# The first expert block's rows, put together on TensorE from the tiles in SBUF instead of read back from DRAM

## The chip, the cores and the metric

The kernel runs on one core of a Trainium2 chip. Its time is the time of the whole launch on the device, in microseconds; lower is better. The kernel before was timed in three runs; the median is what counts. One more execution was taken with the hardware profiler on, and all rows of a profile quoted here come from such an execution.

A core has five engines that run their own instruction streams side by side: PE (TensorE, matrix products; PEld is its weight load), DVE (VectorE), ACT (ScalarE), POOL (GpSimd) and SP (SyncE, which here only issues DMA transfers). They wait for each other by semaphores. SBUF is the core's on-chip memory of 128 partitions, PSUM the memory that PE writes its products to.

## The reference, cut to what matters

Four sequences of 512 tokens with 256 channels. First a gated cross-attention: each token has an index `seg_id` into a context and looks at the four context rows ending there (16 heads of 16 channels). Then a mixture of experts: a gate picks the two best of eight experts for each token.

```python
x = x + tanh(g_xattn[0]) * xattn(layernorm(x), ctx_1024, seg_id, Wq, Wkv, Wo)
# the experts' part, on n = layernorm(x):
gate_probs = softmax(n @ gate_w.T)              # 8 experts
top_v, top_i = top_k(gate_probs, 2)
for e in range(8):
    h = silu(n @ w1[e] + b1[e])                 # 256 -> 1024
    y = h @ w2[e] + b2[e]                       # 1024 -> 256
    out = out + y * comb_w[..., e:e+1]          # top_v where e was picked, else 0
x = x + tanh(g_ffn[0]) * out
```

All data are 32-bit floats.

## The kernel before, in words

**Tiles.** The 2048 tokens are 16 tiles of 128. A tile goes through four stages. `rows_of` has POOL gather its context rows (L240, three buffers). `stage_ask` makes the query: PE `pq` (L426), ACT copies the gate's part (L430). `stage_attend` is DVE work: `prod` (L439, 1024 elements in each partition), its sums (L442), the softmax with ACT's exponent (L459), `v` (L472, written over a buffer of the same kind as `prod`), and sums into `ao` (L483, L485). `stage_out` has PE transpose `ao` (`pa`, L497 or L499), ACT copy it (L512), PE multiply by the output matrix (`po`, L515), and DVE add into `x_sb` (L518) and compute moments for the second normalisation.

**Routing.** Tiles are routed in groups of 2, 2, 1, 1, 1, 1, 2, 2, 2, 2 tiles. `stage_route` stores the tile's `x` (SP, L537), finds the two best experts of each token (DVE; `pick`, L562), counts with two products `pp` over `pick` (L568, L571) how many earlier tokens picked the same expert, and so gives each token a place: `pos` (L604 to L606), a row number in a DRAM array `xs`, which has one region for each expert. ACT takes the exponent for the gate (`exg`, L592) and writes the normalised rows (L609); two scatters on POOL for each tile send them to `xs` (L377). Each row also carries, for each expert, the weight of its result and its token number.

**Queue.** After five tiles (`RAMP`), and after each further group, `queue(i, w)` (L660 to L738) works out, from counts that PE sums (`pn`, L666), which blocks of 128 rows of one expert are sure to be full by now, and which expert and first row each of the next `w` blocks has. DVE does this in some twenty small instructions. Three blocks (0, 1, 2) are sure after five tiles, two more after each of tiles 5, 6 and 7, four more after each pair that follows. 37 blocks are run.

**Blocks.** For each block SP reads the expert and the row number, loads the first-layer weight (`w1s`, L752, three buffers, 1 MB), the biases (L756, L758), the rows `xg` (L770) and their weights `ms` (L773); a load of rows waits until all scatters that can hold its rows have landed. PE transposes the rows (`pxg`, L783), DVE copies them to SBUF (`xgT`, L786), PE makes the hidden layer (`ph`, L798, 32 matrix records), ACT applies Silu (L810, eight instructions), PE makes the result (`py`, L825, 16 records), DVE scales it (`yw`, L836) and POOL adds it to the tokens' rows in the output (L839, an indirect DMA that adds).

**Who sets the order.** The program is written as tiles first, blocks after; a scheduler at build time sorts each engine's instructions by their dependencies and priorities, so attention and blocks interleave on PE, ACT, POOL and SP, in an order that is fixed before the kernel starts. DVE's order for the tiles' part is the written one (`in_order`). In the main loop at index `i` this is: the first half of tile `i`'s attention, the output stage of tile `i - 1`, the question of tile `i + 1`, the routing of the group that ends at `i`, the queue, then (for `i` from 5 on) the rest of tile `i`'s attention:

```python
if i >= RAMP and queued:
    queue(i, queued - before)
    before = queued
...
if i in (0, RAMP, RAMP + 2):
    normalise_first(1 + (i + 1) // TPB)
for _ in attend:
    pass
```

At `i == RAMP` (5) tiles 0 to 4 have been routed and the first three blocks are known; the rest of tile 5's attention follows on DVE.

Of the kernel before, what the change touches and what calls it, by code (L numbers as in the profile page):

```python
# [9 lines left out]
F32 = mybir.dt.float32  # L10
I32 = mybir.dt.int32
U32 = mybir.dt.uint32
AF = mybir.ActivationFunctionType
ALU = mybir.AluOpType
AX = mybir.AxisListType

P = 128
KW = 4
# [5 lines left out]
def gated_xattn_moe(  # L24
# [25 lines left out]
    nc = tc.nc  # L50
    NTOK, D = x.shape
# [3 lines left out]
    KD = D // P  # L55
# [112 lines left out]
    def iota_f(name, shape, pattern, base=0, cm=0):  # L168
        t_i = const.tile(shape, I32, name=name + "_i")
        nc.gpsimd.iota(t_i, pattern=pattern, base=base, channel_multiplier=cm)  # L170
        t_f = const.tile(shape, F32, name=name)
        nc.gpsimd.tensor_copy(t_f, t_i)
        return t_f
# [4 lines left out]
    jfull = iota_f("jfull", [P, NJ], [[P, NJ]], base=P)  # L178
    jany = iota_f("jany", [P, NJ], [[P, NJ]], base=1)
    sid = iota_f("sid", [P, NS], [[1, NS]])  # L180
    srow = iota_f("srow", [P, NS], [[P, NS]])
    tokid = const.tile([P, NT + 1], I32, name="tokid")
    nc.gpsimd.iota(
# [168 lines left out]
    def _layers(ctx, is_near):  # L352
# [18 lines left out]

        scatters, reads = [], []

        def scatter(rows, where):
# [56 lines left out]
        def stage_attend(t):  # L433

            pq = ops.pop(t)
            gt = gathered.pop(t)
            prod = att.tile([P, KW, D], F32, tag="prod", name=f"prod_{t}", bufs=3)
            sc = small.tile([P, KW, H], F32, tag="sc", name=f"sc_{t}")
            seen[t] = nc.vector.tensor_tensor(  # L439
                prod, pq[:, 0:D].unsqueeze(1).to_broadcast([P, KW, D]), gt[:, :, 0:D], ALU.mult  # L440
            ).ins
            nc.vector.tensor_reduce(  # L442
                sc.rearrange("p o h -> p (o h)"),
                prod.rearrange("p o (h d) -> p (o h) d", d=HD),
                AX.X,
                ALU.add,
            )
            yield

            nc.vector.tensor_tensor(  # L450
                sc, sc, neg[:, t, :].unsqueeze(2).to_broadcast([P, KW, H]), ALU.add
            )
            mx = small.tile([P, H], F32, tag="mx", name=f"mx_{t}")
            nc.vector.tensor_reduce(mx, sc.rearrange("p o h -> p h o"), AX.X, ALU.max)
            nc.vector.tensor_tensor(
                sc, sc, mx.unsqueeze(1).to_broadcast([P, KW, H]), ALU.subtract
            )
            ex = small.tile([P, KW, H], F32, tag="ex", name=f"ex_{t}")
            exps[t] = nc.scalar.activation(ex, sc, AF.Exp, scale=rsa[:, t : t + 1]).ins  # L459
            yield  # L460
            sm = small.tile([P, H], F32, tag="sm", name=f"sm_{t}")
            nc.vector.tensor_reduce(sm, ex.rearrange("p o h -> p h o"), AX.X, ALU.add)
            rc = small.tile([P, H], F32, tag="rc", name=f"rc_{t}")
            nc.vector.reciprocal(rc, sm)
            pr = small.tile([P, KW, H], F32, tag="pr", name=f"pr_{t}")
            nc.vector.tensor_tensor(
                pr, ex, rc.unsqueeze(1).to_broadcast([P, KW, H]), ALU.mult
            )
            yield

            v = att.tile([P, KW, D], F32, tag="prod", name=f"v_{t}", bufs=3)
            nc.vector.tensor_tensor(  # L472
                v.rearrange("p o (h d) -> p o h d", d=HD),
                gt[:, :, D : 2 * D].rearrange("p o (h d) -> p o h d", d=HD),
                pr.unsqueeze(3).to_broadcast([P, KW, H, HD]),
                ALU.mult,
            )
            if t + 1 < RAMP:

                ops[t] = v  # L480
                yield
                return
            nc.vector.tensor_add(v[:, 0:2, :], v[:, 0:2, :], v[:, 2:4, :])  # L483
            ao = att.tile([P, 1, D], F32, tag="ao", name=f"ao_{t}")
            nc.vector.tensor_add(ao[:, 0, :], v[:, 0, :], v[:, 1, :])  # L485
            ops[t] = ao
            yield
# [42 lines left out]
        def stage_route(g):  # L530
# [70 lines left out]
            nc.vector.tensor_tensor(  # L601
                hot, hot, place.unsqueeze(2).to_broadcast([P, GT, TOPK, E]), ALU.mult
            )
            pos = gate.tile([P, GMAX, TOPK], I32, tag="pos", name=f"pos_{g}")[:, 0:GT]  # L604
            with nc.allow_low_precision("row numbers"):
                nc.vector.tensor_reduce(pos, hot, AX.X, ALU.add)  # L606
            nc.vector.scalar_tensor_tensor(nm, mv[:, :, 0], -1.0, rs, ALU.mult, ALU.mult)
            rows_in = [
                nc.scalar.activation(  # L609
# [25 lines left out]
            yield  # L635


        ready = []
        done = []
        stores = []  # L640
# [19 lines left out]
        def queue(tiles, w, last=False):  # L660
# [59 lines left out]
            if last:  # L720
                nc.vector.tensor_copy(behind_sure, ends[0:1, E - 1 : E])

                nc.vector.tensor_scalar(
                    row, row, float(E * CAP), None, ALU.min
                )
            else:
                nc.vector.tensor_scalar(took[:, 1 : E + 1], ends, float(w), None, ALU.min)
                take = gate.tile([P, E], F32, tag="take", name=f"take_{q}")
                nc.vector.tensor_tensor(take, took[:, 1 : E + 1], took[:, 0:E], ALU.subtract)
                nc.vector.scalar_tensor_tensor(  # L730
                    issued, take, float(P), issued, ALU.mult, ALU.add
                )
                nc.vector.scalar_tensor_tensor(
                    nextrow, take, float(P), nextrow, ALU.mult, ALU.add
                )
            for i in range(w):
                ready.append((len(ready), q, expert[0:1, i : i + 1], row[0:1, i : i + 1]))
                done.append((len(scatters), len(stores)))  # L738


        why = "entries name experts and rows of their regions"
# [19 lines left out]
        def fetch_rows(s, queued, expert, row, be_v):  # L761
            br_v = nc.values_load(
                row,
                engines=[SP],
                min_val=0,
                max_val=E * CAP,
                skip_runtime_bounds_check_because=why,
            )
            xg = ffn.tile([P, D], F32, tag="xg", name=f"xg_{s}")
            reads_rows(nc.sync.dma_start(out=xg, in_=xs[bass.ds(br_v, P), 0:D]).ins, done[s][0])  # L770
            ms = ffn.tile([P, 2], F32, tag="ms", name=f"ms_{s}", bufs=6)
            reads_rows(
                nc.sync.dma_start(  # L773
                    out=ms, in_=xs[bass.ds(br_v, P), bass.ds(be_v * 2 + D, 2)]
                ).ins,
                done[s][0],
            )
            return xg, ms
# [69 lines left out]
            adds[s] = acc  # L848
            return middle

        weights, rows, turned, pending, outs, adds = {}, {}, {}, [], {}, {}

        def fetch(s):
            if s < limit[0] and s not in rows:
# [28 lines left out]
                return down(*pending.pop())  # L883

        AHEAD = 2
        limit = [MOST]
        if is_near:

# [8 lines left out]
        for i in range(NT + 1):  # L897
            if i + AHEAD < NT:
                gathers.append(rows_of(i + AHEAD))
            attend = stage_attend(i) if i < NT else iter(())  # L900
            queued = surely(i) if i in ends else 0
            with in_order():

                next(attend, None)
                if i != RAMP:
                    next(attend, None)
                if i < RAMP:
                    for _ in attend:
                        pass
                if i:  # L910
                    stage_out(i - 1)
                if i + 1 < NT:
                    stage_ask(i + 1)
                if i in ends:
                    for _ in stage_route(ends[i]):
# [3 lines that stand above are left out]
                    before = queued  # L919
                if i == NT:  # L920
                    queue(i, NS - before, last=True)
                if i in (0, RAMP, RAMP + 2):
                    normalise_first(1 + (i + 1) // TPB)
                for _ in attend:
                    pass
            if is_near and i == 0:
                for b in range(1, B):
                    project_near(
                        kv_near[:, b, :], ps_m, src_rest[:, :, b - 1, :], b, after=exps[0]
                    )  # L930
            if i < E // 2:

                loads = [load_xT(i + 1), load_x(i + 2)] if i + 2 < B else []
                if i + 2 == B:
                    loads.append(load_xT(i + 1))
                for e in (2 * i, 2 * i + 1):
                    loads.append(nc.sync.dma_start(out=w2_sb[:, ts(e, NF), :], in_=w2[ts(e, P), :]).ins)
                for load in loads:
                    behind(load, seen[i], dep=SYNC)
# [91 lines left out]
```

## Time and profile before

| | |
|---|---|
| median of the three runs | 398.99 us (397.70 to 399.93) |
| the profiled execution's own time | 399.22 us |
| its span (first to last instruction) | 397.5 us |
| mean granted clock of TensorE | 0.942 of full speed |
| ACT busy | 160.1 us (40%) |
| POOL busy | 131.3 us (33%) |
| moved by DMA | 94.22 MB, 237 GB/s over the span |
| 32 scatters of rows to `xs` (L377, POOL) | 1.094 us each on POOL |
| 37 loads of rows (L770) | median 5.5 us from issue to landing |

How to read a profile: the busy line gives for each engine the time in which it executed something. The rows of digits cut the span into 40 equal slices (9.94 us each); a digit is the busy share of the slice in tenths, 9 for 90% and more; PEclk is the clock that the chip grants to TensorE, in tenths of full speed. The view of waits sums, for each group of instructions, the idle time of the engine just before them and names what ended it. In a timeline each row is one instruction or a run of like ones: its start (us), its length, its engine and line, the operation with its operands (written before `<-`, read behind it), shapes, and how many; brackets hold the wait just before it and what released it. L798 is line 798 of the kernel before. SPq and POOLq are an engine's issuing of DMAs.

### The profile page before, as it was taken

Reading aid. Unit: us, or ns where it says so; the run is one execution under the profiler, and the core shown is the slowest. Engines: PE = TensorE matmul, PEld = TensorE weight load, DVE = VectorE, ACT = ScalarE, POOL = GpSimd, SP = SyncE. Lnnn points to the kernel's source line nnn. Section 1 sums busy time; section 2 is a strip of 40 time slices with the busy share of each in tenths; the row PEclk is TensorE's granted clock in tenths of the full one; section 3 lists DMA queues with packets and bytes.
Section 4 is the critical chain, followed back from the end, with each engine's and each line's share of the span. In section 5 each row is a group of like instructions: output and inputs, shape, how many; then the busy total and the mean of one; then the engine's idle time right before and its main releaser. Section 6 shows DMA issues by size and latency. Waiting matters only on the chain. (4 is left out here: it accounts for less than half of the span.)

```text
span 397.5 us, 7304 instructions
## 1 busy us (share of the span) xinstructions
PE 343.4 (86%) x2153; PEld 306.9 (77%) x2153; DVE 195.7 (49%) x663; ACT 160.1 (40%) x445; POOL 131.3 (33%) x164
## 2 busy tenths in 40 slices
PE   4877646089999989999999999999999999999960
PEld 1545534078998989898889989999999999999950
DVE  2288797879789989798947301101111111111000
ACT  1121202027756666767576334234243342342410
POOL 4421444513365354453724322112112122121311
PEclk9869696579999999999999999999999999999995
DMA  7899999589969988987667897776767767755111
GB/s 259 269 399 423 419 425 378 177 287 313 299 187 343 237 274 280 336 238 233 205 158 189 281 222 234 236 196 164 246 176 211 214 171 235 195 167 143 18 28 17
DMA packets 43577, 94.22 MB, mean 237 GB/s; under 512 B 14844, under 2 KB 31996, under 8 KB 35720
## 3 DMA queue, kind: packets, MB, share of 16 engines
q1 hardware_dynamic: 33506, 66.23, 51.2%
q0 software_dynamic: 9168, 26.09, 23.0%
q10 hardware_dynamic: 854, 1.33, 1.0%
q8 instruction: 21, 0.34, 0.3%
q14 instruction: 28, 0.23, 0.2%
HBM read 79.90 MB, written 13.73 MB: 236 GB/s over the span
## 5 line engine op out<-in xcount | busy, mean ns | idle before, releaser
L798 PE MATMUL ph<-xgT,w1s 128*128 128x128 f32 x1184 | 143.0, 276 | 0.0
L798 PEld LDWEIGHTS ph<-xgT,w1s 128*128 128x128 f32 x1184 | 140.3, 192 | 2.3
L825 PE MATMUL py<-w_sb,hT 128*128 x592 | 135.7, 380 | 1.4 <-DVE yw L836 0.7
L810 ACT ACTIVATE hT<-ph,b1s 128x128 f32<-128x128 f32 x296 | 83.6, 372 | 113.6 <-issue 95.7
L825 PEld LDWEIGHTS py<-w_sb,hT 128*128 128x128 f32 x592 | 109.2, 190 | 15.7 <-issue 2.1
L839 POOL DMA_INDIRECT out<-yw,ms x37 | 58.7, 1586 | 158.3 <-issue 69.5
L836 DVE SCALAR_TENSOR_TENSOR yw<-py,ms,b2s 128x256 f32<-128x256 f32 x37 | 17.8, 482 | 76.3 <-PE py L825 72.4
L786 DVE COPY xgT<-pxg 128x256 f32<-128x256 f32 x37 | 15.6, 421 | 69.5 <-PE pxg L783 69.4
L377 POOL DMA_INDIRECT xs<-rows,pos x32 | 35.0, 1094 | 30.6 <-ACT rows L609 7.3
L240 POOL DMA_INDIRECT g<-near,idx_near x16 | 17.6, 1098 | 37.4 <-DVE v L472 23.3
L439 DVE TENSOR_TENSOR prod<-pq,g 128x1024 f32<-128x1024 f32 x16 | 19.4, 1213 | 5.9 <-DMA g<-near,idx_near 5.9
L426 PE MATMUL pq<-wqg_sb,xT_sb 128*128 128x264 f32 x64 | 20.5, 449 | 1.5 <-DVE prod L439 1.1
L515 PE MATMUL po<-wo_sb,aoT 128*128 128x264 f32 x64 | 19.8, 436 | 2.0 <-ACT aoT L512 1.4
L472 DVE TENSOR_TENSOR v<-g,pr 128x1024 f32<-128x1024 f32 x16 | 19.6, 1224 | 0.5
L810 ACT ACT_TABLE_LOAD x13 | 16.7, 1283 | 7.7 <-issue 5.2
L442 DVE TENSOR_REDUCE sc<-prod 128x64 f32<-128x1024 f32 x16 | 19.5, 1217 | 0.4
L868 ACT ACTIVATE b2s<-b2s,ms 128x256 f32<-128x256 f32 x37 | 19.5, 532 | 0.0
L426 PEld LDWEIGHTS pq<-wqg_sb,xT_sb 128*128 128x128 f32 x64 | 14.0, 225 | 5.2 <-DVE prod L439 2.2
L497 PE MATMUL pa<-ident,ao 128*128 128x128 f32 x24 | 5.6, 308 | 13.2 <-DVE ao L485 13.1
L515 PEld LDWEIGHTS po<-wo_sb,aoT 128*128 128x128 f32 x64 | 12.1, 207 | 5.6 <-ACT aoT L512 4.0
L783 PE MATMUL pxg<-ident,xg 128*128 128x128 f32 x74 | 14.5, 278 | 1.5 <-DMA xg<-xs 1.5
L497 PEld LDWEIGHTS pa<-ident,ao 128*128 128x128 f32 x24 | 3.3, 165 | 14.5 <-issue 11.6
(128 smaller groups left out, 262.6 us busy)
## 6 DMA issues: line engine op xcount, KB each, us to landing
w1s<-in_w SPq DMA_DIRECT2D x37, 1024.0 KB, 5.4
w_sb<-in_w SPq DMA_DIRECT2D x8, 1024.0 KB
b2s<-in_b SPq DMA_DIRECT2D x37, 128.0 KB, 5.2
xg<-xs SPq DMA_DIRECT2D x37, 128.0 KB, 5.5
xT_sb<-in_xT SPq DMA_DIRECT2D x4, 512.0 KB, 11.3
x_sb<-in_x SPq DMA_DIRECT2D x4, 512.0 KB
out<-x_sb SPq DMA_DIRECT2D x6, 256.0 KB
xs<-padrow SPq DMA_DIRECT2D x9, 136.0 KB, 3.7
```

Source lines behind the costliest of these rows:

```text
L377: i = nc.gpsimd.indirect_dma_start(out=xs, out_offset=bass.IndirectOffsetOnAxis(ap=where, axis=0), in_=rows, in_offset=None,).ins
L426: nc.tensor.matmul(pq, xT_sb[:, t, k, :], wqg_sb[:, k, :], start=(k == 0), stop=(k == KD - 1))
L439: seen[t] = nc.vector.tensor_tensor(prod, pq[:, 0:D].unsqueeze(1).to_broadcast([P, KW, D]), gt[:, :, 0:D], ALU.mult).ins
L442: nc.vector.tensor_reduce(sc.rearrange("p o h -> p (o h)"), prod.rearrange("p o (h d) -> p (o h) d", d=HD), AX.X, ALU.add,)
L472: nc.vector.tensor_tensor(v.rearrange("p o (h d) -> p o h d", d=HD), gt[:, :, D : 2 * D].rearrange("p o (h d) -> p o h d", d=HD), pr.unsqu ...
L515: nc.tensor.matmul(po, aoT[:, k, :], wo_sb[:, k, :], start=(k == 0), stop=(k == KD - 1))
L798: m = nc.tensor.matmul(ph[:, i, :], w1s[:, k, ts(f, P)], xgT[:, k, :], start=(k == 0), stop=(k == KD - 1),).ins
L810: hidden = nc.scalar.activation(hT[:, f, :], ph[:, i, :], AF.Silu, bias=b1s[:, f : f + 1]).ins
L825: m = nc.tensor.matmul(py, hT[:, f, :], w2_sb[:, bass.ds(be_v * NF + f, 1), :].rearrange("p o d -> p (o d)"), start=(f == 0), stop=(f == N ...
L836: outs[s] = nc.vector.scalar_tensor_tensor(yw, py, ms[:, 0:1], b2s, ALU.mult, ALU.add).ins
L839: acc = nc.gpsimd.indirect_dma_start(out=out, out_offset=bass.IndirectOffsetOnAxis(ap=ms[:, 1:2].bitcast(I32), axis=0), in_=yw, in_offset= ...
L868: behind(nc.scalar.activation(b2s, b2s, AF.Copy, scale=ms[:, 0:1]).ins, hidden)
```

## The change

After the queue at `i == RAMP`, a new function `assemble()` builds block 0's transposed rows without DRAM. The routing of the first three groups (tiles 0 to 4) keeps its `pos` tiles and its normalised rows in SBUF (`placed`; three `pos` buffers in place of two), and the queue keeps its row numbers (`row_of`). DVE subtracts block 0's first row number from each token's two places, adds a large number where the difference is negative, and takes the smaller: `at`, the token's place within block 0 if it is below 128. One comparison with `slot` (0 to 127 in each partition) makes `goes`, five 128x128 matrices of ones and zeros. PE multiplies each tile's normalised rows by its matrix and sums the five products in PSUM, for each half of the channels: ten products. The result has the layout that the transposition `pxg` gave. DVE copies it to `xgT_0`; in DVE's written order this copy stands after `normalise_first` and ahead of the rest of tile 5's attention.

Block 0's `xg` load is dropped; its `ms` load stays, and its rows are scattered to `xs` as before. `prod` and `v` share two buffers in place of three. POOL makes `slot` at the start with the other constants. `turned` is defined earlier, since block 0's entry is put there before the blocks begin.

```diff
+    slot = iota_f("slot", [P, P], [[1, P]])
...
+        placed = []
...
-            prod = att.tile([P, KW, D], F32, tag="prod", name=f"prod_{t}", bufs=3)
+            prod = att.tile([P, KW, D], F32, tag="prod", name=f"prod_{t}", bufs=2)
...
-            v = att.tile([P, KW, D], F32, tag="prod", name=f"v_{t}", bufs=3)
+            v = att.tile([P, KW, D], F32, tag="prod", name=f"v_{t}", bufs=2)
...
-            pos = gate.tile([P, GMAX, TOPK], I32, tag="pos", name=f"pos_{g}")[:, 0:GT]
+            pos = gate.tile([P, GMAX, TOPK], I32, tag="pos", name=f"pos_{g}", bufs=3)[:, 0:GT]
...
+            if t0 < RAMP:
+                placed.append((t0, GT, pos, row))
...
+            row_of.append(row[:, 0:1])
...
+        def assemble():
+
+            far_off = float(2 * E * CAP)
+            dist = gate.tile([P, RAMP, TOPK], F32, tag="dist", name="dist", bufs=1)
+            for t0, GT, pos, _ in placed:
+                nc.vector.tensor_tensor(
+                    dist[:, t0 : t0 + GT],
+                    pos,
+                    row_of[0].unsqueeze(2).to_broadcast([P, GT, TOPK]),
+                    ALU.subtract,
+                )
+
+            off = gate.tile([P, RAMP, TOPK], F32, tag="off", name="off", bufs=1)
+            nc.vector.tensor_scalar(off, dist, 0.0, far_off, ALU.is_lt, ALU.mult)
+            nc.vector.tensor_add(dist, dist, off)
+            at = gate.tile([P, RAMP], F32, tag="at", name="at", bufs=1)
+            nc.vector.tensor_reduce(at, dist, AX.X, ALU.min)
+            goes = att.tile([P, RAMP, P], F32, tag="goes", name="goes", bufs=1)
+            nc.vector.tensor_tensor(
+                goes,
+                slot.unsqueeze(1).to_broadcast([P, RAMP, P]),
+                at.unsqueeze(2).to_broadcast([P, RAMP, P]),
+                ALU.is_equal,
+            )
+            px = ps_x.tile([P, KD, P], F32, tag="x", name="pxg_0")
+            tokens = [(t0 + j, row[:, j, :]) for t0, GT, _, row in placed for j in range(GT)]
+            for k in range(KD):
+                for t, row in tokens:
+                    nc.tensor.matmul(
+                        px[:, k, :],
+                        row[:, ts(k, P)],
+                        goes[:, t, :],
+                        start=(t == 0),
+                        stop=(t == RAMP - 1),
+                    )
+            return px
...
-            xg = ffn.tile([P, D], F32, tag="xg", name=f"xg_{s}")
-            reads_rows(nc.sync.dma_start(out=xg, in_=xs[bass.ds(br_v, P), 0:D]).ins, done[s][0])
+            xg = None
+            if s not in turned:
+                xg = ffn.tile([P, D], F32, tag="xg", name=f"xg_{s}")
+                reads_rows(nc.sync.dma_start(out=xg, in_=xs[bass.ds(br_v, P), 0:D]).ins, done[s][0])
...
+                if i == RAMP:
+                    px = assemble()
                 if i in (0, RAMP, RAMP + 2):
                     normalise_first(1 + (i + 1) // TPB)
+                if i == RAMP:
+                    turned[0] = ffn.tile([P, KD, P], F32, tag="xgT", name="xgT_0")
+                    nc.vector.tensor_copy(turned[0], px)
```

## The prediction

> **What bounds it now.** I read the page first, then who waited for whom on PE, then the timelines of PE, DVE, ACT, POOL and SP from 60 to 165 us, each question sending me to the next.
>
> ```profile
> PE 343.4 (86%) x2153; PEld 306.9 (77%) x2153; DVE 195.7 (49%) x663; ACT 160.1 (40%) x445; POOL 131.3 (33%) x164
> PE   4877646089999989999999999999999999999960
> DVE  2288797879789989798947301101111111111000
> PEclk9869696579999999999999999999999999999995
> ```
>
> A slice is 9.9 us. PE is full from slice 8 (about 80 us) to 385 us and nearly empty in slice 7. So time is won by giving PE work before 80 us, and lost by any later PE idling. DVE is almost full beside it until slice 20: PE's later work hangs on a second engine with little to spare.
>
> ```profile
> engine line waited for: us in total, times, longest us
> PE pa L497 <- DVE ao L485: 11.6, 3, 10.7
> PE pxg L783 <- DMA xg<-xs: 1.0, 1, 1.0
> PE pp L568 <- DVE pick L562: 0.4, 1, 0.4
> PE py L825 <- ACT hT L810: 0.3, 1, 0.3
> ```
>
> That is PE from 75 to 150 us. One wait of 10.7 us, then almost none; the same view from 150 us on sums to 3.2 us. The place itself, in PE's timeline:
>
> ```profile
> 68.76 0.37 PE L666 MATMUL pn<-run,all_one 128*128 128x8 f32 x2
> 79.80 0.66 PE L497 MATMUL pa<-ident,ao 128*128 128x128 f32 x2 [10.67 <-DVE ao L485]
> 81.41 0.69 PE L783 MATMUL pxg<-ident,xg 128*128 128x128 f32 x2 [0.95 <-DMA xg<-xs]
> 81.89 1.97 PE L515 MATMUL po<-wo_sb,aoT 128*128 128x264 f32 x4
> 83.65 1.75 PE L426 MATMUL pq<-wqg_sb,xT_sb 128*128 128x264 f32 x4
> 85.24 1.28 PE L798 MATMUL ph<-xgT,w1s 128*128 128x128 f32 x10
> ```
>
> Block 0's first product starts at 85.24. Its rows went through DRAM: SP asked for them at 79.32, when the last scatter (issued by POOL until 73.67) had landed, and they came at 81.4.
>
> **The front of the block stream.** DVE ends the queue (L733) at 73.19. The new code follows there: three small subtractions, compare, add, minimum: six instructions of 0.15 to 0.18 us like their neighbours, about 1.0 us with the gaps, and the 640-wide comparison. No row has that size; 512 wide takes 0.69 us (L483), 1024 wide 1.22 us (L439), on the line between them 0.82. The matrices are ready at about 75.05. Ten 128x128 products are twenty records. At full clock one is 0.112 us (108.27 to 111.84 for 32 of L798), at half twice that. Half throughout gives 4.5 us, an end at 79.5.
>
> Here the clock matters. The granted clock in the trace is 0.50 from 71.3 to 85.0 us, and its changes lie on multiples of 3.41 us (67.9, 71.3, 85.0). The Trainium skill, "TensorE: Matmul & The Clock Gate", Part 1, says the gate looks at free-running windows of 3413 ns and releases after one sustained busy window; it speaks of one idle window as enough to throttle. Read loosely, any start in a window would be released at its end, 78.14. The trace is stricter: the window at 23.5 to 26.9 was busy 2.7 of 3.4 us and released nothing, the one at 64.5 to 67.9 was busy 2.9 us and did. Mine would be busy 3.1 us (75.05 to 78.14), so I take the release at 78.14: products end at 78.8, copy (0.42 us, L786) and two handovers of 0.1, first `ph` at 79.4 at full clock. If the release comes one window later, the front is 1.0 us worse.
>
> Is the weight there by then? SP issues it at 72.40 as before, and the DMA view moves 20 and 0 GB/s in the two microseconds from 78: it has landed.
>
> So `ph` starts 5.8 us earlier. But `pa`, `po`, `pq` of tile 5, which lay before it, now come after it: 0.22 + 0.89 + 0.89 = 2.0 us at full clock (114.01 to 115.79). The net gain at the front is **3.8 us** (2.8 with the later release).
>
> **What is free.** The `slot` iota and its copy, at most 0.5 us, lie on POOL beside a 1.97 us wait before L642. Two `prod` buffers for three make `v` of a first tile wait for PE's reading of the last `v`: worst case, tile 1, PE had read by 31.0 and `v` starts at 32.6; without that 1.5 us it would delay everything one for one. The third `pos` buffer costs memory only. SP drops one load of 0.33 us and some register work, so block 1's weight leaves about 1 us earlier. The output stores are the same in number; SP's place for tile 6's store (it waited 4.6 us there for DVE) moves behind block 3's rows: a small relief, contained below.
>
> **What is queued behind the new wait.** In DVE's order the copy of the new product stands ahead of the rest of tile 5's attention. That rest began at 75.24; now it waits for PE and begins at about 79.3. With 1.9 us of new work and 2.1 us of PE wait, DVE is 4 us late from here, and so are `ao` of tile 5 (79.65, now 83.7), its `v`, hence POOL's gather of tile 8, and tile 5's routing. PE works on block 0 meanwhile and meets `ao` with about 0.3 us of waiting.
>
> The price comes later. PE's order is fixed at build time, and in the built order of the changed kernel PE is further into the blocks when a tile is routed. Routing decides which rows the next blocks read, so I count PE's own work between a routing product (`pp`) and the first transposition (`pxg`) which needs its rows, from the two built orders and the costs above (`py` 0.216 a record: 104.82 to 108.27 for 16):
>
> - tile 5 to block 3: 16.8 us before, 11.3 after;
> - tile 6 to block 5: 21.8, now 13.9; tile 7 to block 7: 22.9, now 16.5;
> - tiles 8 and 9 to block 9: 20.7, now 12.4. The routing stands inside block 7's `ph` where it stood inside block 6's, so one block (7.2 us) of cover and tile 11's three products are missing.
>
> Against that, the rows' trip through DRAM:
>
> ```profile
> 139.78 0.37 PE L568 MATMUL pp<-pick,upto 128*128 128x16 f32 x2 [0.38 <-DVE pick L562]
> ...
> 149.69 0.97 POOL L377 DMA_INDIRECT xs<-rows,pos  x1 [0.30 <-issue]
> ...
> 152.52 0.33 SPq L770 DMA_DIRECT2D xg<-xs  x1
> ```
>
> From `pp` to SP's request for block 9 is 12.74 us. ACT writes the rows after eight Silus in both orders, and POOL issues an output addition and four scatters in both. Landing is not shown here; where PE waited for it, it took 2.05 us (79.32 to 81.4) and 3.4 (228.03 to 231.44), the page's median of those recorded is 5.5. I take 3.4, the wait on a busy DMA. 12.7 + 3.4 - 12.4 = **3.7 us** of PE wait; 2.4 and 5.8 by the ends.
>
> Block 3: ACT's order changes: tile 5's rows, which followed `exg` directly (87.75), now stand behind block 1's eight Silus. From `pp`: 0.7 us of PE, ten products of L798 2.2, last four Silus and handover 1.2, rows 0.7, two scatters 2.4, their landing, the load 3.4. Scatters landed between 1.8 us (150.66 to 152.5) and 6.4 (122.94 to 129.4) after POOL's last; I take 3.8, the one of a single tile on a busy DMA (110.06 to 113.85). Sum 14.4, less 11.3 of work and 0.4 of waiting elsewhere: **2.7 us**; 0 and 7 by the ends. For block 5 ACT's order is kinder (rows before the Silus), so I expect nothing; for block 7 cover suffices.
>
> Small DVE waits (tiles 6 and 7, up to 0.8 us each) were 0.3 each; I add **0.9 us**.
>
> **Sum.** -3.8 + 2.7 + 3.7 + 0.9 = +3.5 us. The profiled execution took 399.22 us (span 397.5 and 1.7 around it): 402.7. That execution is 0.23 above the median 398.99, so the median comes to **402.5 us**.
>
> **Rivals.** (a) *The stream just starts earlier.* If rows land before PE asks, at block 9 within 12.4 us of `pp` and at block 3 within 11.3, only the front counts: 399.0 - 3.8 = 395.2. For it: before, PE waited for `xg` only twice, 1.5 us in all. Against it: these trips had 17 to 23 us of cover then; the 12.74 us to block 9's request alone is more than the new cover. (b) *A draw.* Shortest landings, 2.05 and 1.8: block 3 waits nothing, block 9 about 1.8 to 2.4, with 0.6 of small waits: about 398. (c) *Long landings.* With 5.5 us per load and 4.7 per scatter (the medians of the DMA view) both waits grow by 2 to 4 us, and blocks 1 and 2 wait too, about 1 us each: 408. Against it: with 5.5 us block 17 would have waited over 2 us before, and it waited 0.52. (d) *It does nothing*: if block 0 waited for its weight or ACT's table (1.28 us, 88.37) instead. The DMA view and ACT's idle stretch from 76 to 80 speak against.
>
> **How the numbers follow.** A measurement of this kernel tells about 0.5% (2 us) from no change. My case, waits of 4 to 8 us at blocks 3 and 9: 0.50. (c) 0.10. (b) 0.24. (a) and its neighbours below 397: 0.14. (d) 0.02. The likeliest case lies between 400.5 and 405; its low edge and (b) are within 0.5%: 0.27; slower 0.58; faster 0.15. The range reaches from (a)'s edge, 397, nearly to (c): 408.
>
> **What would show it.** In the changed profile: PE's first `pxg` at 75 us from DVE's `goes`, block 0's `ph` at 79 to 80, full clock from 78.1; then PE waiting for DMA `xg` at about 103 us (2 to 3 us) and 160 us (3 to 5 us). If these two waits are absent, (a) was right; if DVE reaches `goes` later than 75.5 or the clock stays at half to 85, the front is wrong; if PE waits for `ao` for microseconds, DVE became the bound and my sum missed it.

## The result and the profile after

The changed kernel takes 409.53 us (median of 408.26 to 410.57) against 398.71 us for the kernel before: 1.027 times as long, with an interval of 1.0225 to 1.0312. The forecast was 402.5 us, range 397 to 408. Executions over 1.5% above the fastest of the same kernel are left out of the ratios, here and below, but not out of the medians. The profiled execution took 409.0 us, its span is 407.2 us; the lines of the changed kernel have numbers 1 to 51 higher than before (L828 is the transposition that was L783, L870 the result product that was L825).

The page of the changed kernel, the same four lines as were shown of before:

```profile
PE 349.0 (86%) x2171; PEld 309.9 (76%) x2171; DVE 197.7 (49%) x670; ACT 162.5 (40%) x447; POOL 130.0 (32%) x166
PE   4776646499899998599999999999999999999970
DVE  2288797688697989439996541101111011111100
PEclk9969695599999999699999999999999999999995
```

A slice is now 10.2 us. Slice 7 (71 to 81 us) has the work that the change put there: 4 for 0. But slice 16 (163 to 173 us), which was full, shows PE half busy, DVE dropping with it, and a granted clock of 0.6. The view of waits of PE from 75 to 180 us names it:

```profile
PE pxg L828 <- DMA xg<-xs: 7.8, 3, 5.4
PE pxg L774 <- DVE goes L764: 5.5, 1, 5.5
PE pa L499 <- DVE ao L487: 1.5, 4, 0.7
```

The wait for tile 5's `ao` (10.7 us before) is gone. Its place is taken half by the wait for the matrices (5.5), which is earlier, and then three waits for rows come up that were not there. PE's timeline, at the front and then at block 9:

```profile
76.24 4.50 PE L774 MATMUL pxg<-goes,rows 128*128 128x128 f32 x20 [5.46 <-DVE goes L764]
81.26 3.84 PE L843 MATMUL ph<-xgT,w1s 128*128 128x128 f32 x32 [0.52 <-DVE xgT L974]
...
106.38 0.41 PE L828 MATMUL pxg<-ident,xg 128*128 128x128 f32 x2 [2.03 <-DMA xg<-xs]
...
148.00 0.36 PE L570 MATMUL pp<-pick,upto 128*128 128x16 f32 x2
...
151.42 3.62 PE L870 MATMUL py<-w_sb,hT 128*128 x16
...
167.02 0.66 PE L828 MATMUL pxg<-ident,xg 128*128 128x128 f32 x2 [5.41 <-DMA xg<-xs]
167.59 6.20 PE L870 MATMUL py<-w_sb,hT 128*128 x16
173.62 0.38 PE L499 MATMUL pa<-ident,ao 128*128 128x128 f32 x2
```

Block 0 starts 4.0 us earlier (81.26 for 85.24). At block 9 PE stands for 5.41 us, and the 16 result products after it take 6.20 us, where the same 16 took 3.62 us in the block before (151.42 to 155.04). The windows over that place show the clock (columns: stretch, its length, busy time of PE, PEld, DVE, ACT and POOL with counts, granted clock, DMA share, GB/s):

```profile
162.00:165.50 3.50, 0.00 (x0) 0.00 (x0) 1.20 (x1) 1.73 (x7) 2.40 (x2) 1.00 0.95 307
165.50:172.50 7.00, 5.48 (x14) 4.22 (x15) 4.51 (x8) 0.00 (x0) 0.00 (x0) 0.52 1.01 351
172.50:176.00 3.50, 3.50 (x21) 3.09 (x20) 0.29 (x1) 1.88 (x3) 0.00 (x0) 0.98 0.90 347
```

So the wait costs twice: 5.4 us of standing, and then 6.8 us at half clock (165.8 to 172.6), which cost 2.6 us at the result products and 0.3 at the transpositions (0.66 for 0.38): 2.9 us. And while block 9's rows are on their way, the DMA engines are full (0.95, 1.01).

The trip of the rows of tiles 8 and 9, on ACT, POOL and SP of the changed kernel:

```profile
150.94 2.18 ACT L855 ACTIVATE hT<-ph,b1s 128x128 f32<-128x128 f32 x8
152.96 1.14 ACT L613 ACTIVATE rows<-x_sb,nm,rs 128x256 f32<-128x256 f32 x2
...
154.38 2.01 POOL L379 DMA_INDIRECT xs<-rows,pos  x1 [2.79 <-DVE xgT L831]
...
159.25 0.96 POOL L379 DMA_INDIRECT xs<-rows,pos  x1 [0.31 <-issue]
...
162.30 0.33 SPq L815 DMA_DIRECT2D xg<-xs  x1
```

From `pp` (148.00): rows at 153 to 154, last scatter issued by 160.2, request at 162.3, rows there at 167.0. That is 19.0 us, against 13.6 us that PE had to do between `pp` and the transpositions (148.0 to 161.6, a wait of 0.7 us for `ao` among them).

The cover is short because the routing is late. PE comes to block 9's transpositions at the same time as before (161.61 us; 161.57 in the kernel before): four microseconds of lead at block 0 are used up by then, by tile 5's products, which now come after it, and by the wait at block 3 (and tile 11's three products, which were done by then before, are still to come). But DVE picks the experts of tiles 8 and 9, just ahead of `pp`, 8.2 us later. The first line is before, the second after:

```profile
139.46 0.17 DVE L562 TENSOR_TENSOR pick<-hot 128x16 f32<-128x16 f32 x1
147.68 0.17 DVE L564 TENSOR_TENSOR pick<-hot 128x16 f32<-128x16 f32 x1
```

Of these 8.2 us, 5.9 were there when tile 5's `ao` was begun (85.14 for 79.22): 1.3 from before the assembly, 1.7 for the assembling instructions, 2.9 for the wait for PE and the copy. The other 2.3 us came between tile 5 and tiles 8 and 9.

Where the time went, by the instants when each block's result is scaled (`yw`): the changed kernel is 0.3 us ahead at block 6, 9.9 us behind at block 7 (whose products are the 6.20 us row), and 9.8 us behind from block 16 to the end.

### The profile page after: what moved, and what is told of

Its sections match the earlier page's. It is cut to its first block, busy times and chain, and to the rows that moved or that the text cites. A ratio compares the mean times of both kernels' runs of the same rounds, so it can differ in the third digit from the quotient of the medians.

```text
span 407.2 us, 7348 instructions
## 1 busy us (share of the span) xinstructions
PE 349.0 (86%) x2171; PEld 309.9 (76%) x2171; DVE 197.7 (49%) x670; ACT 162.5 (40%) x447; POOL 130.0 (32%) x166
## 5 line engine op out<-in xcount | busy, mean ns | idle before, releaser
L870 PE MATMUL py<-w_sb,hT 128*128 x592 | 139.4, 385 | 1.1 <-DVE yw L881 0.7
L870 PEld LDWEIGHTS py<-w_sb,hT 128*128 128x128 f32 x592 | 110.5, 193 | 15.9 <-issue 2.4
L379 POOL DMA_INDIRECT xs<-rows,pos x32 | 34.3, 1073 | 39.0 <-DVE upb L692 10.2
L428 PE MATMUL pq<-wqg_sb,xT_sb 128*128 128x264 f32 x64 | 19.2, 428 | 3.3 <-DVE prod L441 2.9
L828 PE MATMUL pxg<-ident,xg 128*128 128x128 f32 x72 | 14.2, 279 | 8.3 <-DMA xg<-xs 8.2
L514 ACT COPY aoT<-pa 128x256 f32<-128x256 f32 x16 | 6.1, 383 | 30.8 <-PE pa L499 25.2
L428 PEld LDWEIGHTS pq<-wqg_sb,xT_sb 128*128 128x128 f32 x64 | 12.9, 207 | 6.6 <-DVE prod L441 4.1
L828 PEld LDWEIGHTS pxg<-ident,xg 128*128 128x128 f32 x72 | 9.0, 145 | 9.8 <-issue 8.0
```

Of the source, the lines that this page charges most:

```text
L379: i = nc.gpsimd.indirect_dma_start(out=xs, out_offset=bass.IndirectOffsetOnAxis(ap=where, axis=0), in_=rows, in_offset=None,).ins
L428: nc.tensor.matmul(pq, xT_sb[:, t, k, :], wqg_sb[:, k, :], start=(k == 0), stop=(k == KD - 1))
L828: nc.tensor.transpose(px[:, k, :], xg[:, ts(k, P)], ident)
L870: m = nc.tensor.matmul(py, hT[:, f, :], w2_sb[:, bass.ds(be_v * NF + f, 1), :].rearrange("p o d -> p (o d)"), start=(f == 0), stop=(f == N ...
```

## The experiments

Theory A: the loss is an order. In PE's stream, fixed at build time, a tile's routing stands further into the blocks; the rows' trip through DRAM is then longer than the work that covers it. Theory B took other forms: the assembly itself, DVE's lateness after it, or the side parts. Ratios are to the kernel before, timed beside each run, with 95% intervals.

**The side parts alone.** The kernel before with two `prod` buffers, three `pos` buffers and the `slot` constant:

```diff
+    slot = iota_f("slot", [P, P], [[1, P]])
-            prod = att.tile(..., bufs=3)
+            prod = att.tile(..., bufs=2)
-            pos = gate.tile([P, GMAX, TOPK], I32, tag="pos", name=f"pos_{g}")[:, 0:GT]
+            pos = gate.tile([P, GMAX, TOPK], I32, tag="pos", name=f"pos_{g}", bufs=3)[:, 0:GT]
```

> The kernel before with only the side parts of the change: two buffers for prod and v in place of three, three for pos in place of two, and the slot constant on POOL; no assembly. In the changed kernel's profile everything from 12 us on was 0.8 to 1.1 us late. Theory A (that is the chance of where the clock's windows and a DMA's landing fell): 398.7 us, within 0.5. Theory B (the side parts cost it): 399.8 us, with the first question product at 13.9 us for 13.1 and DVE 0.9 us late at 47 us.

Measured 399.43 us, ratio 1.0024 (1.0008 to 1.0040): 1.0 us, so B held here, and "free" in the prediction was wrong by that. Of it 0.2 us can be placed: from tile 1's `v` to the `pp` of tiles 2 and 3 it is 29.24 us where it was 29.03. The lateness at 12 us was not there in this profile (`v` of tile 1 at 32.71 us for 32.56; 33.40 in the changed one), so most of the 0.8 to 1.1 us seen after the change was chance of that execution. Where the other 0.8 us of this run's 1.0 arise was not found.

**Block 9's transpositions later on PE.**

```diff
+            late = s + 1 in (9,)
+            if late:
+                middle = finish()
             if s + 1 < limit[0]:
                 turned[s + 1], copy = turn(s + 1, rows[s + 1][0])
-            middle = finish()
+            if not late:
+                middle = finish()
```

> The changed kernel, with block 9's transpositions set behind block 7's result products on PE (before: ahead of them). Theory A (the loss is PE standing 5.4 us at block 9's transpositions because too little work lies between the routing of tiles 8 and 9 and them, and then 6.9 us at half clock, which costs 2.8 us more): the 3.6 us of result products now cover part of the wait, about 1.8 us of it stays, too short for the clock to fall; 409.5 - 3.6 - 2.8 = 403 us, PEclk 0.9 or more in the slices after 160 us. Theory B (DVE, 4 us late since tile 5, is what PE really waits for, and the wait at block 9 is only where it shows): the time stays within 1 us of 409.5, with the same microseconds of waiting at other products.

Measured 405.8 us, ratio 1.0168 (1.0124 to 1.0212): about 4 us better than the change, where A gave 6.4 and B nothing. The wait at block 9 is on the path; how much of the rest is given away again at other waits differs by execution (402.5 to 407.1 us).

**Filling the wait, first try.**

```diff
+            if s == 9:
+                for _ in range(24):
+                    nc.tensor.transpose(px[:, 0, :], ident, ident)
```

> The changed kernel, with 24 transpositions of the identity, whose result is overwritten, set just ahead of block 9's transpositions: 48 records of 0.112 us, 5.4 us of work for PE in the time in which it stood still. It tells the wait and the clock apart. Theory A (the half clock after 165.6 us comes of the standing still and costs 2.8 us by itself): the clock stays full and the time falls by 2.8 to 406.7 us. Theory B (the half clock comes at that place whatever PE does, or costs nothing since something else bounds): 409.5 or more, and half clock between 160 and 180 us.

Measured 409.58 us, ratio 1.0283 (1.0238 to 1.0328): no gain. The expectation had its size wrong: a transposition is one record, not two, so the filling was 2.8 us long, 2.7 us of wait stayed, and the clock still fell, for one stretch of 3.4 us. The insertion also moved later tiles' work in PE's order. It decides nothing; it was repeated below with the order held.

**DVE's order turned round.** The copy of the assembled rows behind tile 5's attention:

```diff
-                if i == RAMP:
-                    turned[0] = ffn.tile([P, KD, P], F32, tag="xgT", name="xgT_0")
-                    nc.vector.tensor_copy(turned[0], px)
                 for _ in attend:
                     pass
+                if i == RAMP:
+                    turned[0] = ffn.tile([P, KD, P], F32, tag="xgT", name="xgT_0")
+                    nc.vector.tensor_copy(turned[0], px)
```

> The changed kernel, with the copy of the assembled rows put behind the rest of tile 5's attention on DVE (before: ahead of it). DVE no longer stands 2.5 us waiting for the products, and tile 5 is routed earlier; block 0's first product comes about 2 us later (83 for 81.3 us). Theory A (the losses are the short covers at blocks 3 and 9): block 3's wait of 2.0 us goes, block 9's cover by the built order is about 12.5 us again, so most of its wait of 5.4 and the half clock stay; 407 to 410 us. Theory B (DVE's lateness since tile 5 is the loss): 402 us or less.

Measured 424.39 us in the median and 418.5 at the least (no interval), against 398.33: at least 5% longer. In the median both theories missed by over 10 us. The scheduler made a third PE order of it, with 12.2 us of waits for rows in four places from 75 to 180 us, and half clock again and again. With DVE on time it is the worst kernel here.

**PE's order held.** Two kernels with a list of PE's instructions in the wanted order, each chained behind the one before:

```diff
+        pe_order = "pxg10 pa2 po2 pq2 ph5 pp2 pn1 ph11 pxg2 py3 ph12 pa2 ph3 po2 pq2 ph1 pxg2 py4 pp2 py1 pn1 ..."
+        def keep_order():
...
+                    if last is not None:
+                        behind(made[kind][n], last)
+                    last = made[kind][n]
```

The first is the kernel of the run above, assembly and all, in the order of before:

> The changed kernel with its assembly, but with PE's instructions held to the order they had before the change, from the first block to the last queue (the ten assembling products first, then tile 5's pa, po and a pq, then block 0 and all that follows as before); the copy of the assembled rows stands behind tile 5's attention on DVE. Theory A (what costs is the order: PE is further into the blocks when a tile is routed, and the rows' trip through DRAM is then too long): no wait for rows over 1 us, full clock from block 0 on; block 0 starts at about 86.2 us for 85.2 before, plus 1.0 us that the side parts measured: 400.4 us, within 1.5. Theory B (the assembly itself, or DVE's lateness of it, costs in whatever order PE works): 406 us or more.

Measured 401.74 us against 400.01, ratio 1.0058 (1.0032 to 1.0084): 2.3 us more than before, as A said (1.7). The same kernel without the list took 418.5 us or more. PE's waits from 75 to 180 us hold no wait for rows at all:

```profile
PE pxg L427 <- DVE goes L799: 5.5, 1, 5.5
PE pa L432 <- DVE ao L522: 3.3, 4, 2.0
PE pp L427 <- DVE pick L599: 0.7, 2, 0.4
```

The second is the kernel before, with no assembly, in the order of the change:

> The kernel before, with no assembly (block 0's rows come from DRAM), but with PE's instructions held to the order they have in the changed kernel. Theory A (the order costs): block 0 starts at about 82.5 us, and PE waits for the rows of blocks 3 and 9 as it does in the changed kernel (2 and 5 us), with half clock after the longer wait: 407 us, within 3. Theory B (the assembly costs, the order doesn't): 396 to 400 us, no wait for rows over 1 us.

Measured 414.08 us against 400.01, ratio 1.0346 (1.0299 to 1.0393). Nothing is assembled here, and it loses more than the change. The waits from 75 to 180 us, and block 9 in the timeline:

```profile
PE pxg L430 <- DMA xg<-xs: 20.6, 4, 11.4
```

```profile
152.49 0.29 PE L425 MATMUL pp<-pick,upto 128*128 128x16 f32 x2
...
171.69 0.66 PE L430 MATMUL pxg<-ident,xg 128*128 128x128 f32 x2 [5.66 <-DMA xg<-xs]
172.23 5.64 PE L425 MATMUL py<-w_sb,hT 128*128 x16
```

11.4 us is block 0's own wait, at the place of the old wait for `ao`. The others are 2.0 us at block 3, 1.5 us at block 7 and 5.66 us at block 9, with half clock after it (5.64 for 3.62), as in the changed kernel. The two kernels make a table with the change:

| PE's order | rows of block 0 from DRAM | assembled |
|---|---|---|
| of before | 1 | 1.0058 |
| of the change | 1.0346 | 1.027, 1.0285 |

Down the first column only PE's order differs: it costs 3.5%. So the order alone is enough for such a loss, without assembly and without DVE's copy (DVE begins tile 5's `ao` at 79.15 us there, for 79.22 before; but PE, standing for block 0's rows, serves tile 5 late, and the `pick` of tiles 8 and 9 starts at 151.48). Part of this loss is its own, though: block 0's first layer ran at half clock there, 6.57 us for 3.84 in the changed kernel. Down the second column it is 2.1 to 2.3%, but there two things differ: the kernel in the first row has DVE's copy behind the attention, the one in the second ahead of it. No run has the order of the change with the copy behind; one with nearly the order of before and the copy ahead stands below ("Keeping the early start") and took 1.0179. How the change's 2.7% divides between PE's order and DVE's lateness is therefore not separated. Across the second row the assembly gains 0.6 to 0.8%, across the first it costs 0.6%.

**A shorter trip, by POOL.** POOL writes the normalised rows, and ACT is left out of the trip:

```diff
-                nc.scalar.activation(row[:, j, 0:D], x_sb[:, t0 + j, :], AF.Identity, bias=nm[:, j : j + 1], scale=rs[:, j : j + 1])
+                nc.gpsimd.tensor_scalar(row[:, j, 0:D], x_sb[:, t0 + j, :], mv[:, j, 0:1], rs[:, j : j + 1], ALU.subtract, ALU.mult)
```

> The changed kernel with the normalised rows written by POOL right after it has made the scale (before: by ACT, behind up to eight Silus of a block); PE's order is the changed kernel's but for single places. It shortens the rows' trip and leaves the cover alone. From the changed profile: the first scatter of tiles 8 and 9 could leave at about 152 us for 154.4, and block 3's scatters some 4 us sooner. Theory A (trip longer than cover): block 3's wait goes (2.0), block 9's falls to 3 us or less and with it the half clock (2.8): 402 us, within 2. Theory B (the trip is not what PE waits for in the end): within 1 us of 409.5.

and the control for it, the same edit of the kernel before:

> The control for the run before it: the kernel before, with the rows written by POOL. PE waited for rows only twice there, 1.5 us in all, and the one at block 0 (1.0 us) is followed by work that is waiting anyway. Theory A (a shorter trip is worth something only where its cover is short): 398.3 us, within 1.2. Theory B (POOL's rows help or hurt by themselves, through ACT's or POOL's or DVE's time): a difference of 2 us or more.

Measured 408.39 us against 400.01, ratio 1.0223 (1.0183 to 1.0263), and for the control 402.65, ratio 1.0073 (1.0049 to 1.0096). In its figures A failed (402), and the time lies nearer to B's (409.5); for the control B's held. But the trip to block 9 was 15.7 us (from `pp` at 148.44) for 19.0, and the wait 2.15 us for 5.41: both 3.3 us less, so the trip is what PE waits for there.

```profile
164.06 0.41 PE L827 MATMUL pxg<-ident,xg 128*128 128x128 f32 x2 [2.15 <-DMA xg<-xs]
164.60 5.29 PE L869 MATMUL py<-w_sb,hT 128*128 x16
```

POOL takes twice ACT's 0.6 us for a row:

```profile
L584 POOL TENSOR_SCALAR rows<-x_sb,mv,rs x16: 1208/1222/1263, 42.7 to 228.7; 128x256 f32<-128x256 f32 x16
```

(columns: shortest, median and longest, ns). The control says that POOL's rows cost 2.9 us by themselves. If they cost the same in the changed kernel, which no run shows, the shorter trip gains 1.2 to 1.35% of the time. That is less than the 7.5 us (1.9%) that A gave, in part because the clock fell for 3.4 us even after the wait of 2.15 us.

**A shorter trip, on ACT.** PE's and ACT's orders held to the changed kernel's, but for three places where the rows go ahead of a block's Silus:

```diff
-  "... exg1 hT8 rows1 b2s1 ... exg2 hT8 rows2 b2s1 ... exg2 hT8 rows2 b2s1 ..."
+  "... exg1 rows1 hT8 b2s1 ... exg2 rows2 hT8 b2s1 ... exg2 rows2 hT8 b2s1 ..."
```

> The changed kernel with PE's instructions held to its own order and ACT's too, but for three places: the rows of tile 5, of tiles 8 and 9 and of tiles 12 and 13 are written by ACT right after the gate's exponents, ahead of the eight Silus of a block that stood between. It shortens two trips and leaves PE's order and cover alone. Rows of tiles 8 and 9 are then there about 1.7 us after pp for 5.0. Theory A (the trip against the cover): block 3's wait (2.0 us) goes; block 9's falls from 5.4 to about 2.2 us, the half clock after it to 3.4 us or none; ratio to the kernel before 1.010 for 1.027, between 1.005 and 1.016. Theory B (the trip isn't what PE waits for): 1.025 or more.

Measured 407.1 us against 398.69, ratio 1.0190 (1.0157 to 1.0222): between the theories. The profile is of the slowest of the six executions (408.57 us). Timelines of POOL, SP and PE (`pp` is at 145.46):

```profile
154.12 0.96 POOL L379 DMA_INDIRECT xs<-rows,pos  x1 [0.30 <-issue]
...
159.01 0.09 SPq L868 DMA_DIRECT2D xg<-xs  x1
...
164.75 0.66 PE L432 MATMUL pxg<-ident,xg 128*128 128x128 f32 x2 [5.68 <-DMA xg<-xs]
```

The last scatter is issued 9.6 us after `pp` (12.2 in the changed kernel), but it is 3.9 us more before SP may ask (2.1), and the load takes 5.7 us (4.7). The whole trip is 19.3 us again. From 158 to 162 us the DMA engines are 0.91 to 1.05 busy: a tile's gather of 1 MB and a block's weights are under way with the rows. In this execution what was saved at ACT was given back before the rows landed, so the run doesn't separate the theories. Block 3's wait did shrink to 1.0 us; where the rest of the median's gain on the change, some 3 us in all, comes from was not found.

**Keeping the early start.** Block 0's first layer right behind the assembly, everything later in the order of before, the copy ahead of the attention as in the change, rows early in two places:

```diff
-        pe_order = "pxg10 pa2 po2 pq2 ph5 pp2 pn1 ph11 pxg2 py3 ..."
+        pe_order = "pxg10 ph16 pa2 po2 pq2 pp2 pn1 pxg2 py3 ..."
```

> An attempt to keep the early start: the changed kernel with block 0's first layer right behind the assembly (as the change has it), all later PE work in the order of the kernel before, and the rows of tiles 8 and 9 and of 12 and 13 ahead of the Silus on ACT. Theory A (the start is earlier by some 3 us, but the blocks after it depend on routings that DVE makes no earlier; the slack at block 9 before was the cover of 20.7 less a trip of about 17.4, so 3 us, and about 1 us at block 3): most of the gain is lost again in waits at blocks 3 and 9; ratio 0.995 to 1.005. Theory C (with the order mended the early start is a gain in full): ratio 0.992 or less, no wait for rows over 1 us. Theory B of the runs before (the assembly costs in any order): 1.015 or more.

Measured 406.03 us against 398.69, ratio 1.0179 (1.0139 to 1.0219). A's figure failed, and C's; B's (1.015 or more) is the one that came, although the same assembly had taken 1.0058 above. Block 0's first layer did start early, at 78.27 us. PE hardly waited for rows; it waited for DVE:

```profile
PE pa L432 <- DVE ao L533: 6.1, 5, 3.1
PE pp L427 <- DVE pick L610: 2.3, 2, 2.0
```

The copy ahead of tile 5's attention makes DVE late, and this order of PE expects the tiles at their old times; the longest of these waits, 3.06 us for tile 6's `ao`, was followed by 3.4 us at half clock. That this is the whole of it was not separated. What the run shows is that the order of before, which keeps the assembled kernel near its time when the copy stands behind the attention, does not when it stands ahead and block 0 is moved up: some 6 us of earlier start at block 0 (this execution was 1.0 us ahead already at 67 us) were lost, and more. No version here beats the kernel before.

**The changed kernel once more.**

> The changed kernel once more, unchanged, for a second profile. Theory A: the trip of tiles 8 and 9's rows, from pp to block 9's transpositions, is 18.3 to 19.2 us again, PE waits there 4 us or more and falls to half clock; the 0.8 to 1.1 us of lateness at 47 us is not there again in full. Ratio 1.023 to 1.031.

Measured 411.1 us against 398.69, ratio 1.0285 (1.0242 to 1.0329). Trip of the rows 18.8 us (149.10 to 167.9), wait 5.23 us, half clock for 6.8 us after it: as A said. The lateness at the start did not go away but was larger (`v` of tile 1 at 34.01 us; 33.40 in the first profile, 32.57 in the one with the first filling), which fits chance. Over the profiles of eight runs where PE waited at block 9, the trip measured 18.3 to 19.3 us; only POOL's rows made it 15.7.

**Filling the wait, with the order held.**

```diff
+            if s == 9:
+                for _ in range(40):
+                    tr("pxg", px[:, 0, :], ident, ident)
```

> The changed kernel with PE held to its own order but for 40 transpositions of the identity (80 records, 9.0 us at full clock, their result overwritten) just ahead of block 9's transpositions, so that PE has no idle time there at all: the wait was 5.4 us in one profile and 5.2 in another, and 24 of them left 2.7. Theory A (the half clock after 165.6 us comes of PE's standing still, and costs 2.8 us by itself): block 7's result products after it take 3.6 us for 6.2, PEclk is 1.0 from block 0 to the end of the blocks; the filling costs 9.0 - 5.4 = 3.6 and gains 2.8: ratio 1.029 for 1.027 and 1.0285. Theory B (the half clock comes at that place whatever PE does): half clock between 160 and 180 us, ratio 1.036.

The size was again taken double: the filling is 40 records, 4.5 us. It fits into the wait and costs nothing, so A's ratio is 1.020. Measured 405.7 us against 398.21, ratio 1.0165 (1.0119 to 1.0212): about 4 us faster than the changed kernel, with 40 useless transpositions more to do.

```profile
160.48 4.53 PE L432 MATMUL pxg<-ident 128*128 128x128 f32 x40
166.03 0.44 PE L432 MATMUL pxg<-ident,xg 128*128 128x128 f32 x2 [1.02 <-DMA xg<-xs]
166.55 3.72 PE L427 MATMUL py<-w_sb,hT 128*128 x16
```

```profile
PEclk9969696599999999999999999999999999999995
```

1.02 us of wait is left, and the result products take 3.72 us for 6.20; the clock stays full to the end of the blocks. So the half clock comes of the standing still. Its price can be read apart from the wait's, if only from one profile each: by the instants of `yw`, this kernel is 1.0 us ahead of the changed one at block 6 (158.60 for 159.56) and 3.9 us at the last block (391.19 for 395.13), so 3.0 us arose behind. The 4 us of the ratios can't all be put down to the filling, since no run holds PE's order alone.

## Why the prediction was wrong, point by point

The direction and most of the mechanism were right: block 0 starts earlier, tile 5 later, and PE then waits for rows at blocks 3 and 9, where the sum placed it. The step that failed is the half clock after the wait at block 9, which the sum put at nothing; two other terms, the front and the trip to block 9, were mis-sized. The sum was 3.5 us; the profile has 9.7 us more in its span (407.2 for 397.5). By the terms of the sum:

**The front, -3.8.** It came to -2.0: block 0 at -3.98, then 2.0 us for `pa`, `po`, `pq`. The matrices came at 76.2 us for the forecast 75.05, past the 75.5 that the prediction named as the sign of a wrong front. Everything up to them was 1.0 to 1.3 us later in this execution than before, some of it the side parts that were called free (1.0 us in the median, interval 0.3 to 1.6), the rest, as far as the profiles show, chance. And the clock was released at 80.48 us, not at 78.14: the products took 4.50 us, all at half. The forecast had taken the place of the windows from the one trace of the kernel before; in this one they lie elsewhere (the clock changed at 71.4 and 85.05 us there, at 60.0 and 80.48 here). A later release was the prediction's other case, 1.0 us worse; it came.

**Block 3, 2.7.** It was 2.03 us, and 2.18 in the second profile. The trip was 14.7 us (91.66 to 106.4) for 14.4; the load took 4.8 us for the 3.4 assumed, other parts less.

**Block 9, 3.7.** It was 5.41. This is the mis-sized term: the trip, taken as 12.7 + 3.4 = 16.1 us, was 19.0. The request came 14.3 us after `pp`, ACT began the rows 5.0 us after `pp` for 3.8 before (it stood idle for 1.27 us ahead of the Silus that the rows wait behind; PE makes 22 of the 32 records of those Silus' products after `pp` in this order, 14 before); the load took 4.7 us, while the DMA engines were full. The cover was 13.6 us for the 12.4 counted. Both 3.4 and 12.7 were measured, but in the kernel before, at other places and in another order.

**The clock after a wait, which was not in the sum.** 2.9 us. It is the step that failed: the prediction used the clock gate to price the front, with the rule of the Trainium skill's "TensorE: Matmul & The Clock Gate", Part 1, that one idle window of about 3.4 us is enough to throttle, and then forecast a wait of 3.7 us further on without applying the rule to it. By the rule that wait would bring half clock if a whole window lay in it, and none otherwise. The trace agrees with the page at this place: the clock fell at 165.81 us, and the 3.4 us before that lay wholly in the wait (161.61 to 167.02). It has 6.8 us of half clock with that wait of 5.4, and the last run above shows the price.

**Small waits, 0.9.** They were 0.4 at block 1's rows; the others from 75 to 180 us sum to the same as before (`ao` 0.6 more, `pick` and `hT` 0.6 less). What is left over, 1.1 us, was not placed; it is not in PE's waits after 190 us, which sum to 2.9 us for 2.7 before.

Together: +1.8, -0.7, +1.7, +2.9, -0.5 and +1.1, which is the 6.3 us between forecast and profile (409.0 for 402.7). Of the rivals, (c), long landings at 408, was the nearest, and was given 0.10 with the argument that block 17 had waited only 0.5 us. That argument rested on one place. The range's upper end, 408, was 1.5 us short; with the clock's 2.9 us in the sum it would have reached the result.

Left open: how the loss divides between PE's order and DVE's lateness in the changed kernel, why the scheduler's order changes as it does with a small edit (what is shown is only that it does, with 418.5 or more and 402 us for one set of operations), and what exactly makes the scatters and loads land later when they are issued sooner, beyond that the DMA engines are busy then.

## What to carry to other kernels

When a change lets an engine start sooner, look for what the later work depends on: here the blocks hung on routings that came no sooner, and in the change even later, because the new work stood ahead of them on DVE and in PE's order; a trip through DRAM lost its cover. Where a scheduler sets the order, compare the built orders first, and price a trip by the longest landing that the trace shows on a busy DMA, not by a lucky one. A forecast wait on TensorE of more than about two microseconds can carry a second price, the half clock after it, as one of 2.15 us did here.

## What the runs showed of the hardware

The granted clock fell after shorter waits than expected. Waits of 2.03 and 2.18 us at block 3 left it full, and one of 2.60 us in the first filling (at 247 us); one of 2.15 us and one of 2.71 us at block 9, and one of 3.06 us in the attempt to keep the early start, were each followed by 3.4 us at half; waits of 5.2 to 5.7 us came with 6.8 us of it, twice as much. The page named above speaks of an idle window of about 3.4 us; the three waits of 2.15 to 3.06 us are shorter than that, so the measurement decides: less than a window of idling can be enough, and waits of nearly one length (2.15 and 2.18, 2.60 and 2.71) can end differently.

A 128x256 row on POOL took 1.22 us, on ACT 0.6. And a load of 128 KB took from 2.05 us (before, block 0, asked for at 79.32 us; the DMA engines moved nothing from 79 to 80 us) to 5.7 us (block 9 with the rows early on ACT, while the engines were 0.9 to 1.05 busy).
